# A two-layer graph transformer: order of the last products of a block, the engine of two bias adds, and the place of the last weight sums

## The chip, the cores and the metric

The kernel runs on one core of a Trainium2 chip. The core has five engines with a queue each, and each queue runs in order: TensorE (PE, matrix products into PSUM), VectorE (DVE), ScalarE (ACT), GpSimd (POOL) and SyncE (SP, which here only issues DMAs). The metric is the device time of one launch in microseconds; lower is better.

## The reference

`x` is 2708 x 512, `adj` a sparse symmetric 0/1 matrix of 2708 x 2708 (about 9 ones in a row, the diagonal included). Two layers follow each other, each a graph attention with 8 heads of 64 and a feed-forward part of 2048:

```
q, k, v = h @ Wq.T + bq, h @ Wk.T + bk, h @ Wv.T + bv
scores  = q . k / 8, -1e9 where adj (plus the diagonal) is 0
ctx     = softmax(scores) @ v
h1 = layer_norm(h + ctx @ Wo.T + bo, ln1_g, ln1_b)
ff = relu(h1 @ W1.T + b1) @ W2.T + b2
h2 = layer_norm(h1 + ff, ln2_g, ln2_b)
```

All is in 32-bit floats.

## The kernel before

The program is written engine by engine with a schedule by hand: what stands first in the code stands first in its engine's queue. The 22 tiles of 128 tokens are sorted by number of neighbours. For a tile, POOL gathers the rows of keys and values of each token's neighbours by indirect DMA (`kv`), VectorE multiplies and sums them (L1150, L1156), ScalarE forms the weights `p` and scales the values (L1169, L1176), and VectorE adds (L1182, L1189). This attention runs ahead of the feed-forward part and beside it: the generator `attend` is advanced by `advance` a little in each of the 16 steps f of a feed-forward block, by a table of paces.

A feed-forward block has two tiles, A and B (256 tokens side by side in `hT`). Step f makes 128 hidden units: four products `pf` on PE (L1653), then ScalarE's relu into `ft` (L1664). The main loop puts other work between the steps:

- in f = 5 to 8 the steps of `keys_values` for the block before: transposes of its result `z`, then for each tile the products k and v (`project`, L620). ScalarE copies both out of PSUM (L1735, L1739), POOL adds the bias `bk` to k afterwards (L1745) and then stores the rows by indirect DMA.
- in f = 5 `residuals` gathers the input rows `xb` of the next block; in f = 9 `settled_rows` has POOL add the bias `bo` to them (L1431).
- in f = 10 to 12 `attended` of the next block: transposes of the attention's result `cx`, the projection `o` of each tile on PE, `h = o + xb` on VectorE (L1456), the norm (L1265 to L1279, with a root on POOL, L1275).
- in f = 15 `turned`: eight transposes of these `h` into the next `hT`.

Small products `o`, k, v and transposes share PSUM buffers of the tag g, of which this stage has two.

In layer 0 the blocks 2 to 9 use `feed_forward_by_seven` for the second product with W2. Hidden units 2j and 2j+1 form pair j. For the pairs 0 to 6 the 2 x 2 block product (tokens A, B by the left and right half of the outputs, L and R) is done with seven products of 128 x 128 x 256 instead of eight (a Strassen-Winograd scheme). It needs sums of tokens, formed by VectorE per pair in `sums(j)` (L1625 to L1628, at f = 2j + 2), and sums of weights t2, t3, t4, formed once by `form(j)` in block 1, at the steps 3, 5, 7, 9, 13, 14 and 15, written to DRAM, and fetched anew for each pair of each block (`ask_forms`, L1610) into three fixed places, `self.slots`. These hold one pair, so the fetch for pair j + 1 goes out when the seven products of pair j have read them. The products go into four accumulators: a0, a1 (rows of A and B) and c0, c1 (shared parts). `products(j - 2)` stands at odd f. Pair 7 is plain: two products into a0 (128 x 512) and four into a1 (128 x 256).

A 128 x 128 x 256 product of floats is two PE instructions in the trace.

At a block's end the order on PE is: `pf` of f = 15, `products(5)`, the eight transposes of `turned`, `products(6)`, then the plain pair (L1674, L1678). ScalarE then copies c0's left half (u2, L1695), VectorE combines the accumulators with `h` (L1696 to L1703) and runs both norms. The next block's `pf` follow on PE at once; its `products(0)` stand at its f = 5.

Of the kernel before, what the change touches and what calls it, by code (L numbers as in the profile page):

```python
# [13 lines left out]
ALU = mybir.AluOpType  # L14
# [4 lines left out]
P = 128  # L19
DM = 512  # L20
# [5 lines left out]
NFC = FF // P  # L26
# [457 lines left out]
def by_edges(ctx: ExitStack, tc: tile.TileContext, x, xT, adj, layers, out, redo):  # L484
# [9 lines left out]
    nc = tc.nc  # L494
# [132 lines left out]
    def plus_rest(to, o, r, scale=None):  # L627
        for part in rest(o, r):
            if scale is None:
                nc.vector.tensor_tensor(to, part, to, ALU.add)  # L630
            else:
                nc.vector.scalar_tensor_tensor(to, part, scale, to, ALU.mult, ALU.add)
# [15 lines left out]
    def size(g):  # L648
        return min(P, N - g * P)
# [644 lines left out]
    class Layer:  # L1294
        def __init__(self, n, w):
            self.n, self.w, self.w1, self.w2, self.due = n, w, [], [], None
            self.apart, self.other = True, False
            self.with_bo = n > 0
            self.stores = nc.sync

        def load_first(self):
# [122 lines left out]
                xbs.append(xb)  # L1424
            return xbs

        def settled_rows(self, block, xbs):

            for g, xb in zip(block, xbs):
                r = size(g)  # L1430
                nc.gpsimd.tensor_tensor(xb[:r], xb[:r], self.bo[:r], ALU.add)  # L1431
            self.with_bo = True

        def attended(self, block, got, xbs=None):

            cTs, hs = [], []
            with_bo, self.with_bo = self.with_bo, self.n > 0

            def turn(g):
                r = size(g)  # L1440
                cx = got.pop(g)
                cT = dn.tile([P, NC, P], F32, tag="cT", name="cT", bufs=3)
                flip(cx, r, cT[:, :, :r], self.bv)
                cTs.append((g, r, cT))

            turn(block[0])
            xbs = xbs or self.residuals(block)
            yield
            if block == blocks[0]:
                turn(block[1])  # L1450
                yield
            for i, xb in enumerate(xbs):
                g, r, cT = cTs[i]
                o = project(lambda c: cT[:, c, :r], r, self.wo, "o")
                h = dn.tile([P, DM], F32, tag="h", name="h", bufs=4)
                nc.vector.tensor_tensor(h[:r], o[:r], xb[:r], ALU.add)  # L1456
                plus_rest(h[:r], o, r)
                if not with_bo:
                    nc.vector.tensor_tensor(h[:r], h[:r], self.bo[:r], ALU.add)
                norm(h, r, self.g1, self.e1b2)  # L1460
                hs.append(h)
                if len(cTs) == 1:
                    turn(block[1])
                yield
            yield hs
# [110 lines left out]
        def prepared(self):  # L1576

            place = wts.tile([P, NC, DM], F32, tag="wq", name="forms")
            place = place.rearrange("p c n -> p (c n)")
            W = 2 * P  # L1580
            self.slots = [place[:, i * W : (i + 1) * W] for i in range(3)]
            sums = place[:, 3 * W : 6 * W].rearrange("p (two s t) -> p two s t", two=2, t=P)
            self.sums = [sums[:, i] for i in range(2)]
            self.more_fts = [place[:, i * W : (i + 1) * W] for i in (6, 7)]
            self.asked = 0

        def form(self, j):

            w, W = self.w2[j], 2 * P
            b11, b12, b21, b22 = w[:, 0, :W], w[:, 0, W:], w[:, 1, :W], w[:, 1, W:]  # L1590
            t2, t3, t4 = self.slots
            nc.vector.tensor_tensor(t3, b22, b12, ALU.subtract)
            nc.vector.tensor_tensor(b12, b12, b11, ALU.subtract)
            nc.vector.tensor_tensor(t2, b22, b12, ALU.subtract)
            nc.vector.tensor_tensor(t4, b21, t2, ALU.subtract)
            for i, t in enumerate((t2, t3, t4)):
                nc.sync.dma_start(out=form_d[j, i], in_=t)
# [15 lines left out]
        def feed_forward_by_seven(self, k, block, hs, hT):  # L1613

            J, W = NFC // 2 - 1, 2 * P
            L, R = slice(0, W), slice(W, DM)
            a0, a1 = (ps_a.tile([P, DM], F32, tag=f"a{i}", name=f"a{i}") for i in range(2))
            c0, c1 = (ps_s.tile([P, DM], F32, tag=f"c{i}", name=f"c{i}") for i in range(2))
            fts = []
# [10 lines left out]
            def products(j):  # L1630
                f0, f1, w, s = fts[2 * j], fts[2 * j + 1], self.w2[j], self.sums[j % 2]
                t2, t3, t4 = self.slots
                first, last = j == 0, j == J - 1
                for to, left, right, start, stop in (
                    (a1[:, L], f1[:, P:], t4, first, False),
                    (c0[:, R], s[:, 1], t2, first, False),
                    (c1[:, L], f0[:, P:], t3, first, False),
                    (c0[:, L], f0[:, :P], w[:, 0, L], False, last),
                    (a0[:, L], f1[:, :P], w[:, 1, L], first, False),
                    (c1[:, R], s[:, 0], w[:, 0, R], False, last),  # L1640
                    (a0[:, R], s[:, 2], w[:, 1, R], False, False),
                ):
                    nc.tensor.matmul(to, left, right, start=start, stop=stop)  # L1643
                self.ask_forms(base + min(3 * j + 6, 3 * J + 3 * (k < NB - 2)))
                if k == NB - 2:
                    self.form_back(j)

            self.ask_forms(base + 3)
            for f in range(NFC):
                j = f // 2  # L1650
# [17 lines left out]
                if f % 2 and j > 1:  # L1668
                    products(j - 2)
                yield None  # L1670
            products(J - 1)
            for i in range(2):
                f, w = 2 * J + i, self.w2[J]
                nc.tensor.matmul(a0, fts[f][:, :P], w[:, i, :], start=False, stop=i == 1)  # L1674
            for cols in (L, R):
                for i in range(2):
                    f, w = 2 * J + i, self.w2[J]
                    nc.tensor.matmul(  # L1678
                        a1[:, cols],
                        fts[f][:, P:],  # L1680
                        w[:, i, cols],
                        start=False,
                        stop=(cols is R and i == 1),
                    )
            zA, zB = hs
            u2 = dn.tile([P, W], F32, tag="ft", name="u2", bufs=4)
            u34 = dn.tile([P, DM], F32, tag="row", name="u34", bufs=3)
# [20 lines left out]
        def keys_values(self, block, zs):  # L1708

            n = self.n + 1  # L1710
            kvs = at.tile([P, SLOTS, 2 * DM], F32, tag="kv", name="kvs", bufs=KVB)
            zTs = []

            def turn(i):
                g, z = block[i], zs[i]
                r = size(g)
                zT = dn.tile([P, NC, P], F32, tag="cT", name="zT", bufs=3)
                if r < P:
                    nc.gpsimd.memset(zT, 0.0)
                flip(z, r, zT[:, :, :r], self.nbo)  # L1720
                zTs.append(zT)

            turn(0)
            if block != blocks[-1]:
                turn(1)
            yield
            for i, (g, z) in enumerate(zip(block, zs)):
                r, zT = size(g), zTs[i]
                kv = kvs[:, i, :]
                k = project(lambda c: zT[:, c, :r], r, self.kv[0], "k")  # L1730
                if block == blocks[-1]:
                    nc.vector.tensor_tensor(kv[:r, :DM], k[:r], self.bk[:r], ALU.add)
                    plus_rest(kv[:r, :DM], k, r)
                else:
                    nc.scalar.copy(kv[:, :DM], k)  # L1735
                if len(zTs) == 1:
                    turn(1)
                v = project(lambda c: zT[:, c, :r], r, self.kv[1], "v")
                nc.scalar.copy(kv[:r, DM:], v[:r])  # L1739
                plus_rest(kv[:r, DM:], v, r)  # L1740
                nc.sync.dma_start(out=zT_d[n][g], in_=zT)
                nc.sync.dma_start(out=xb_d[n][g * P : g * P + r, :], in_=z[:r])
                yield
                if block != blocks[-1]:
                    nc.gpsimd.tensor_tensor(kv[:, :DM], kv[:, :DM], self.bk, ALU.add)  # L1745
            for i, g in enumerate(block):
                r = size(g)
                written[n].append(
                    put(kv_d[n], ident_i[:r, g : g + 1], kvs[:r, i, :], f"kv{n}")
                )  # L1750
            yield
# [130 lines left out]
    for n in range(NL):  # L1882
# [47 lines left out]
        for k, block in enumerate(blocks):  # L1930
# [14 lines left out]
            for f, zs in enumerate(working):  # L1945
# [16 lines left out]
                if more and f == NFC - 1:  # L1962
                    finish(asking)
                    hT = now.turned(blocks[k + 1], hs_next)
                if xbs and f == 9 + 2 * (k == 0):
                    now.settled_rows(blocks[k + 1], xbs)
                advance((PACE7 if seven else (PACE if k else PACES)[n])[f])
                if f in (0, 3, 7, 9) and (f or k):
                    next(asking, None)
# [116 lines left out]
```

## Time and profile before

| | us |
|---|---|
| median of 3 runs | 1870.61 (1869.64 to 1870.89) |
| the profiled execution, own time | 1877.7 |
| its span, first to last instruction | 1875.9 |
| stage of the eight seven-product blocks | about 397 to 1052 of the span |

In the profile PE, DVE, ACT and POOL are the engines, PEld is PE's loading of weights. A row of a group gives line, engine, operation, output<-inputs and shapes; "idle before" is how long the engine stood idle right before, and `<-` names what ended the wait. `forms` is the buffer that holds the slots, the token sums and two spare `ft` places, so `DMA forms<-form_d` is a fetch of weight sums, and `DVE forms L1627` a token sum. Line numbers are those of the kernel before; in the changed kernel lines from L1299 on are lower by 1 to 15.

### The profile page before, as it was taken

How to read it: one execution, taken by the hardware profiler on the slowest of the kernel's cores; microseconds unless marked ns; L12 is line 12 of the kernel's file. 1: busy time of each engine (PE TensorE's matmuls, PEld its weight loads, DVE VectorE, ACT ScalarE, POOL GpSimd, SP SyncE). 2: the span in 40 equal slices, each digit the busy share in tenths (PEclk: the TensorE clock that was granted, in tenths of full speed). 3: DMA queues.
4: the chain of work that ended last, by engine and by line, in shares of the span. 5: the costliest groups of instructions: out<-in, count | busy, mean ns of one | idle time of the engine just before them, and what ended most of it. 6: DMA issues, size and time to landing. Idle time of an engine off the chain costs nothing.

```text
span 1875.9 us, 22547 instructions
## 1 busy us (share of the span) xinstructions
PE 1827.0 (97%) x6563; PEld 1169.7 (62%) x6563; DVE 1461.5 (78%) x2407; ACT 960.7 (51%) x3291; POOL 860.4 (46%) x785
## 2 busy tenths in 40 slices
PE   9999999999989999998999999999999999999998
PEld 4444466566667767766776644566666666666666
DVE  5886778888788988878885336887989898998853
ACT  5760445545455565545644213456655675666541
POOL 3234755635454554645552114435544563555402
PEclk9999999999999999999999999999999999999999
DMA  9987976756665675656553568744736563654400
GB/s 345 370 327 270 369 262 229 252 172 212 207 206 181 204 248 195 208 196 193 182 175 110 177 226 326 276 156 160 254 129 226 197 238 131 226 209 165 145 23 21
DMA packets 158062, 393.82 MB, mean 210 GB/s; under 512 B 17514, under 2 KB 60894, under 8 KB 157928
## 3 DMA queue, kind: packets, MB, share of 16 engines
q0 software_dynamic: 70608, 252.12, 39.5%
q1 hardware_dynamic: 77162, 118.55, 18.5%
q10 hardware_dynamic: 10158, 21.61, 3.1%
q8 instruction: 54, 0.88, 0.2%
q14 instruction: 80, 0.66, 0.1%
HBM read 338.78 MB, written 53.44 MB: 209 GB/s over the span
## 4 chain that ended last, share of the span: by engine, by line
PE 48%; DVE 4%; ACT 2%; issue 1%; DMA 1%; POOL 0%; DVEq 0%; POOLq 0%
PE pf L1524 15%; PE a L1497 15%; PE o L620 5%; PE q L620 3%; PE pf L1653 2%; PE k L620 2%; PE v L620 2%; PE c L1643 1%; PE tp L1285 1%; PE a L1643 1%; ACT kv L1176 1%; DVE kv L1150 1%; DVE sc L1156 1%; DVE acc L1189 0%; PE a L1512 0%
## 5 line engine op out<-in xcount | busy, mean ns | idle before, releaser
L1113 POOL DMA_INDIRECT kv<-kv_d,listed x420 | 522.7, 1245 | 272.6 <-issue 93.2
L1524 PE MATMUL pf<-hT,w 128*128 128x256 f32 (+1 forms) x1792 | 393.2, 367 | 0.1
L1524 PEld LDWEIGHTS pf<-hT,w 128*128 128x128 f32 x1792 | 323.5, 190 | 103.2 <-issue 63.4
L1497 PE MATMUL a<-w,ft 128*128 128x512 f32 x800 | 373.1, 592 | 0.0
L1275 POOL TENSOR_TENSOR rd<-va,mhalf 128x1 f32<-128x1 f32 (+1 forms) x88 | 83.5, 948 | 522.3 <-DVE va L1273 522.1
L1176 ACT ACTIVATE kv<-kv,p 128x64 f32<-128x64 f32 x1232 | 311.0, 335 | 5.4
L1150 DVE TENSOR_TENSOR kv<-kv,q 128x1024 f32<-128x1024 f32 (+1 forms) x222 | 257.9, 1162 | 14.6 <-DMA q<-q_d,ident_i 12.9
L1156 DVE TENSOR_REDUCE sc<-kv 128x16 f32<-128x1024 f32 (+1 forms) x222 | 258.0, 1162 | 7.6
L1653 PE MATMUL pf<-hT,w 128*128 128x256 f32 x1024 | 236.8, 384 | 11.2 <-ACT ft L1664 11.2
L1189 DVE TENSOR_TENSOR acc<-acc,kv 128x1024 f32<-128x1024 f32 (+2 forms) x178 | 206.1, 1158 | 37.7 <-ACT kv L1176 21.3
L1653 PEld LDWEIGHTS pf<-hT,w 128*128 128x128 f32 x1024 | 194.6, 192 | 49.9 <-ACT ft L1664 13.4
L1497 PEld LDWEIGHTS a<-w,ft 128*128 128x128 f32 x800 | 150.1, 190 | 113.2 <-issue 101.3
L1535 ACT ACTIVATE ft<-pf,b 128x256 f32<-128x256 f32 (+1 forms) x208 | 95.0, 459 | 200.9 <-PE pf L1524 195.4
L1169 ACT ACTIVATE p<-sc,listed 128x8 f32<-128x8 f32 x420 | 104.4, 297 | 159.0 <-DVE sc L1156 147.1
L620 PE MATMUL o<-wo,cT 128*128 128x512 f32 x336 | 153.3, 600 | 8.4 <-DVE h L1456 6.7
L1182 DVE TENSOR_TENSOR kv<-kv,p 128x512 f32<-128x512 f32 (+1 forms) x178 | 130.5, 733 | 27.5 <-ACT p L1169 27.4
L1664 ACT ACTIVATE ft<-pf,b 128x256 f32<-128x256 f32 x96 | 44.7, 467 | 146.9 <-PE pf L1653 146.9
L620 PEld LDWEIGHTS o<-wo,cT 128*128 128x128 f32 x336 | 63.4, 192 | 85.4 <-issue 72.5
L745 DVE MAX8 tops<-code 128x8 f32<-128x247 f32 (+2 forms) x242 | 78.5, 400 | 28.0 <-ACT code L740 28.0
L1279 DVE SCALAR_TENSOR_TENSOR h<-h,rd,ln_b 128x512 f32<-128x512 f32 (+1 forms) x88 | 66.1, 751 | 42.5 <-POOL rd L1275 42.5
L1220 ACT ACTIVATE cx<-acc,su 128x64 f32<-128x64 f32 (+1 forms) x352 | 88.2, 333 | 15.3 <-DVE flags L1804 7.5
L1176 ACT ACTIVATE acc<-kv,p 128x64 f32<-128x64 f32 (+1 forms) x352 | 88.8, 334 | 1.4
(234 smaller groups left out, 2344.0 us busy)
## 6 DMA issues: line engine op xcount, KB each, us to landing
aj<-in_adj SPq DMA_DIRECT2D x42, 677.0 KB, 6.0
forms<-form_d SPq DMA_DIRECT2D x168, 128.0 KB, 3.6
kv_d<-kvs ACTq DMA_DIRECT2D x21, 512.0 KB, 5.4
xg<-in_xT SPq DMA_DIRECT2D x19, 512.0 KB, 7.6
w<-in_W SPq DMA_DIRECT2D x16, 512.0 KB, 6.8
kv<-kv_d,listed POOLq DMA_INDIRECT x420, 6.1
zT_d<-zT SPq DMA_DIRECT2D x22, 256.0 KB, 3.4
xb_d<-h SPq DMA_DIRECT2D x21, 256.0 KB, 4.6
```

Of the source, the lines that this page charges most:

```text
L620: nc.tensor.matmul(o[:r], xs(c), wm[:, c, :], start=(c == 0), stop=(c == NC - 1))
L1113: return nc.gpsimd.indirect_dma_start(out=to, out_offset=None, in_=table[:, :], in_offset=bass.IndirectOffsetOnAxis(ap=s, axis=0), bounds_ ...
L1150: nc.vector.tensor_tensor(kv[:r, :c, :DM], kv[:r, :c, :DM], self.q[:r].unsqueeze(1).to_broadcast([r, c, DM]), ALU.mult,)
L1156: nc.vector.tensor_reduce(self.sc[:r, s0 : s0 + c, :], kv[:r, :c, :DM].rearrange("p s (h d) -> p s h d", d=DK), AX.X, ALU.add,)
L1169: nc.scalar.activation(p[:r, s, :], self.sc[:r, s, :], AF.Exp, bias=minus[:r, g, s : s + 1])
L1176: nc.scalar.activation(to[:, i, hd], kv[:r, i, DM + h * DK : DM + (h + 1) * DK], AF.Copy, scale=p[:r, s0 + i, h : h + 1],)
L1182: nc.vector.tensor_tensor(to[:, 0, :].rearrange("p (h d) -> p h d", d=DK), kv[:r, 0, DM:].rearrange("p (h d) -> p h d", d=DK), p[:r, s0, : ...
L1189: nc.vector.tensor_tensor(self.acc[:r, :c, :], self.acc[:r, :c, :], kv[:r, :c, DM:], ALU.add)
L1497: nc.tensor.matmul(a[:r, cols], fts[f][:, c0 : c0 + r], self.w2[f // 2][:, f % 2, cols], start=(f == 0), stop=(f == NFC - 1),)
L1524: nc.tensor.matmul(pf[:, :w], self.w1[f // 2][:, c, f % 2 * P : f % 2 * P + P], hT[:, c, :w], start=(c == 0), stop=(c == NC - 1),)
L1535: nc.scalar.activation(ft[:, :w], pf[:, :w], AF.Relu, bias=self.b1[:, f : f + 1])
L1653: nc.tensor.matmul(pf[:, :W], self.w1[j][:, c, f % 2 * P : f % 2 * P + P], hT[:, c, :], start=(c == 0), stop=(c == NC - 1),)
```

## The change

Three things are changed.

1. In `feed_forward_by_seven` the plain pair's six products move ahead of `products(6)`; the flags that end an accumulation move with them.
2. The bias `bo` is no longer added to `xb` by POOL: `settled_rows` is gone, and in layer 0 VectorE adds `bo` to `h` for all blocks (before: the first block only). The bias `bk` is added by VectorE while it takes k out of PSUM, for all blocks (before: the last block only); ScalarE's copy of k and POOL's add go.
3. `form(6)` writes its sums to the three places where the token sums lie (`other_slots`), not to `self.slots`.

```diff
-            self.with_bo = n > 0
...
-        def settled_rows(self, block, xbs):
-            for g, xb in zip(block, xbs):
-                r = size(g)
-                nc.gpsimd.tensor_tensor(xb[:r], xb[:r], self.bo[:r], ALU.add)
-            self.with_bo = True
...
-                if not with_bo:
+                if self.n == 0:
                     nc.vector.tensor_tensor(h[:r], h[:r], self.bo[:r], ALU.add)
...
+            self.other_slots = [place[:, i * W : (i + 1) * W] for i in range(3, 6)]
...
-            t2, t3, t4 = self.slots
+            t2, t3, t4 = self.slots if j < NFC // 2 - 2 else self.other_slots
...
-                    (a1[:, L], f1[:, P:], t4, first, False),
+                    (a1[:, L], f1[:, P:], t4, first, last),
...
-                    (a0[:, R], s[:, 2], w[:, 1, R], False, False),
+                    (a0[:, R], s[:, 2], w[:, 1, R], False, last),
...
-            products(J - 1)
             for i in range(2):
                 f, w = 2 * J + i, self.w2[J]
-                nc.tensor.matmul(a0, fts[f][:, :P], w[:, i, :], start=False, stop=i == 1)
+                nc.tensor.matmul(a0, fts[f][:, :P], w[:, i, :], start=False, stop=False)
             for cols in (L, R):
...
-                        stop=(cols is R and i == 1),
+                        stop=False,
                     )
+            products(J - 1)
...
-                if block == blocks[-1]:
-                    nc.vector.tensor_tensor(kv[:r, :DM], k[:r], self.bk[:r], ALU.add)
-                    plus_rest(kv[:r, :DM], k, r)
-                else:
-                    nc.scalar.copy(kv[:, :DM], k)
+                nc.vector.tensor_tensor(kv[:r, :DM], k[:r], self.bk[:r], ALU.add)
+                plus_rest(kv[:r, :DM], k, r)
...
-                if block != blocks[-1]:
-                    nc.gpsimd.tensor_tensor(kv[:, :DM], kv[:, :DM], self.bk, ALU.add)
...
-                if xbs and f == 9 + 2 * (k == 0):
-                    now.settled_rows(blocks[k + 1], xbs)
```

More of the change, by code (lines that the diff above doesn't have):

```diff
@@ L1425, in residuals @@
             return xbs
-        def settled_rows(self, block, xbs):
-            for g, xb in zip(block, xbs):
-                r = size(g)
-                nc.gpsimd.tensor_tensor(xb[:r], xb[:r], self.bo[:r], ALU.add)
-            self.with_bo = True
         def attended(self, block, got, xbs=None):
             cTs, hs = [], []
-            with_bo, self.with_bo = self.with_bo, self.n > 0
             def turn(g):
```

## The prediction

> **What bounds the kernel now.** The page's first part comes first: which engine fills the span.
>
> ```profile
> PE 1827.0 (97%) x6563; PEld 1169.7 (62%) x6563; DVE 1461.5 (78%) x2407; ACT 960.7 (51%) x3291; POOL 860.4 (46%) x785
> ```
>
> TensorE (PE) sets the time. The change removes none of its products, so it can gain only where PE stands still or runs slowly. I cut the stage that it touches, the layer-0 blocks by seven products (397 to 1052 us), into its blocks (block ends read from the timeline of PE); columns: length, busy time of PE, PEld, DVE, ACT and POOL, granted clock, DMA share, GB/s.
>
> ```profile
> 316.40:397.00 80.60, 80.60 (x277) 50.03 (x276) 69.07 (x100) 44.62 (x164) 43.13 (x36) 1.00 0.68 220
> 481.60:567.10 85.50, 79.97 (x311) 58.06 (x310) 68.44 (x108) 41.79 (x153) 44.81 (x34) 0.96 0.60 193
> 567.10:644.20 77.10, 75.99 (x311) 56.61 (x311) 68.21 (x107) 43.80 (x162) 44.71 (x36) 1.00 0.69 226
> 807.00:892.40 85.40, 78.72 (x312) 57.64 (x311) 71.14 (x108) 46.00 (x171) 43.23 (x35) 0.98 0.59 186
> ```
>
> The plain block before (first row) has no idle PE. The seven-product blocks all have the same products, yet last from 77.1 to 85.5 us, and the long ones also had a lower clock. The waits of PE in 395 to 1052 us say on what (us in total, times, longest):
>
> ```profile
> PE pf L1653 <- ACT ft L1664: 11.2, 7, 3.6
> PE a L1643 <- DMA forms<-form_d: 9.9, 6, 2.7
> PE o L620 <- DVE h L1456: 6.7, 5, 2.4
> PE c L1643 <- DVE forms L1627: 4.1, 3, 2.9
> PE c L1643 <- DMA forms<-form_d: 2.3, 3, 1.1
> ```
>
> And the timeline of PE at one block's end shows where (start, us, what, idle before):
>
> ```profile
> 553.15 0.59 PE L1643 MATMUL a<-w,forms 128*128 128x256 f32 x2
> 553.58 1.04 PE L1285 MATMUL tp<-ident,h 128*128 128x128 f32 x8
> 556.46 0.89 PE L1643 MATMUL a<-forms,ft 128*128 128x256 f32 x2 [1.84 <-DMA forms<-form_d]
> 558.29 1.19 PE L1643 MATMUL c<-forms 128*128 128x256 f32 x2 [0.94 <-DMA forms<-form_d]
> ...
> 561.14 1.06 PE L1643 MATMUL a<-w,ft 128*128 128x256 f32 x2
> 561.99 1.06 PE L1643 MATMUL c<-w,forms 128*128 128x256 f32 x2
> 562.85 1.01 PE L1643 MATMUL a<-w,forms 128*128 128x256 f32 x2
> 563.69 1.88 PE L1674 MATMUL a<-w,ft 128*128 128x512 f32 x4
> 565.41 1.89 PE L1678 MATMUL a<-w,ft 128*128 128x256 f32 x8
> ```
>
> The last seven wait for weight sums that are fetched into slots which the seven before only just released: 0.87 us of transposes is all that lies between. After the wait PE starts a product every 0.85 us instead of 0.43, for some 4 us. The plain pair (3.44 us, needing no fetched sums) stands behind, where it covers nothing.
>
> **Part 1, the order of products.** One end without a wait is 0.87 of transposes, 7 x 0.43 and 3.44: 7.3 us, as the last two blocks show (965.20 to 972.54 and 1044.60 to 1051.91). The other six take 10.31, 13.55, 8.61, 9.47, 11.35 and 12.02 us: 21.3 over in all. Of this 12.4 is the waits themselves (11.4 on DMA, 1.0 on VectorE's token sums), the rest mostly half rate. In the new order the first sum is wanted 3.44 us later than the transposes' end, the next ones 0.43 and 0.86 after it. Against the landings seen: block of 556.46 wants at 557.89, its t2 that landed by 558.29 at 558.32; that of 884.04 at 884.65; that of 475.91 (third sum) at 476.48; the others have 1.3 us or more. So all are covered, three with 0.6 us or less to spare. Landings of these loads run from 1.8 to 6.3 us, so I charge 1.0 for one that comes late. The plain pair needs ft of f = 15: in the tightest block it ends at 797.02 and is wanted at 797.38. No charge. The moved step also issues, on SP's queue, the three fetches for the next block's first pair (in the last such block a reload of weights): 3.44 us later, for products that PE wants 10.4 us after the end; the landing of 3.5 (median) fits, and the stores behind them in the queue are waited for by nobody in this stage. No charge.
>
> Here the Trainium skill (TensorE: Matmul & The Clock Gate, "What's actually happening") weighs differently: the array falls to half clock after an idle window of about 3.4 us. No gap here is that long (the longest single one 2.66, two near each other 2.78 together), so by the rule each gap costs its own length: 12.4 us. By the row it costs 21.3. I take the row; the half-rate stretches at 558 and at 884 us follow gaps of 0.9 to 2.7 us.
>
> The price is the block's tail. The four accumulators used to be emptied partly beneath the plain pair; the last add chain began 0.2 us after the block's end E (481.82 against 481.62). Now c0's left half is ready at E - 1.1, ScalarE's copy takes 0.41 to reach VectorE, and the adds of the rows L1696 to L1700, each 0.33 to 0.61 apart, put L1701 at E + 1.87: 1.67 later. Behind it on VectorE stand the two norms, then the token sums of the next block's first pair, which PE wants at E + 10.8. Their third sum ended at E + 8.3 (489.92), so E + 10.0: 0.8 us of cover is left. Without it each boundary would wait.
>
> **Part 2, the biases.** POOL loses 20 adds of 1.38 us and 20 of 1.28; ScalarE 20 copies of 0.586. VectorE gains 20 of 0.69 (row of h<-h,bo) and 20 of 0.69 (kvs<-k,bk, which the last block has already): 27.6 us. But POOL's adds hold VectorE up. The timelines of POOL and of VectorE:
>
> ```profile
> 534.53 2.82 POOL L1431 TENSOR_TENSOR xb<-xb,bo 128x512 f32<-128x512 f32 x2
> ```
>
> ```profile
> 534.86 1.36 DVE L1625 TENSOR_TENSOR forms<-ft 128x128 f32<-128x128 f32 x1
> 536.26 1.25 DVE L1626 TENSOR_TENSOR ft<-ft 128x128 f32<-128x128 f32 x1
> 537.42 0.28 DVE L1627 TENSOR_TENSOR forms<-forms,ft 128x128 f32<-128x128 f32 x1
> ```
>
> Adds of 0.28 us took 1.36 and 1.25: 2.0 lost, just ahead of L1456, which frees the PSUM buffer that the second o projection waits for (at 538.85, 1.03). The same 2.0 to 2.1 stands ahead of the waits of 0.90, 0.19 and 2.21; another POOL add costs 1.55 (L1628, 1.84 for 0.29). Four waits go or nearly go: -4.3. The fifth (2.36, with 1.7 of half rate behind it) I leave: in that block VectorE never rests between the k adds and L1456, and 1.4 to 2.1 added meets 2.6 taken away.
>
> Each bo add lengthens the chain from o to the transposes of h by 0.69; those h are ready 2.7 us or more before PE wants them (632.93 against 635.62 is the closest), so nothing. A k add waits for PE's k. Queued behind it are scores and weights; but in seven of the eight blocks VectorE already waits 2 to 7 us there for ScalarE's p, which stands behind the copy of v, later than k. So its wait costs between 0 and, where nothing waits yet, 0.69; nothing, by the rows. It also frees k's PSUM buffer, which the next k wants 8.2 us after. In the block starting at 567.13 VectorE gets there at E + 26.6, with the tail E + 28.2, done at 28.9, while PE comes at 28.0: +1.0. The block from 892.4 already waits 0.18 for token sums: +1.0. ScalarE's lost copies are worth nothing, for the copy of v behind waits for PE anyway (31.1 us in 12 waits). Nor are POOL's: VectorE waits for no gather of keys in this stage.
>
> **Part 3, sums of the last pair.** The forming at 397.80 shows no wait, so other slots free nothing on VectorE. The first fetch can leave earlier; PE's 0.76 wait at 404.13 goes, but the wait of 2.87 behind it is for token sums and takes its place: 0, or -0.76 if it weren't so. Those sums are one bo add later: +0.7.
>
> **The sum**, on the profiled execution (1877.7 us, span 1875.9): -21.3 + 1.0 - 4.3 + 1.0 + 1.0 + 0.7 = -21.9. The median of the runs, 1870.61, is 7 us shorter; I take the same difference off it: 1849.
>
> **Rivals.** Forecast (0.80): most of the 21.3 is got; 1841 to 1861. The low end has all costs nought (-3.7) and the fifth o wait gone (-4.1); the high end has two thirds of the waits back in smaller size.
>
> Fetches stay late (0.09): if the ask meets busier queues and lands 2 us later, six ends still wait 1 to 1.5 us, partly with 1.7 of half rate: 12 to 15 given back, 1861 to 1865. For: the three margins. Against: SP's queue asks at the same point as before.
>
> The tail becomes the wait (0.11). PE would stop at the next block's first products, a place with 0.8 us of cover. If VectorE is 1.8 us later than I reckon, each of seven boundaries waits 1.0 and may add 1.7 of half rate: 19 given back, 1868, no change (0.06). From 2.8 us on, gaps of 2 us and half rate give back 26 and more: 1875 to 1880, slower (0.05). For: VectorE is 80 to 88% busy here. Against: its locks go, and POOL stands idle for the norms' reciprocal roots.
>
> POOL's locks not the cause: only the 4.3 is lost, 1853, within the forecast.
>
> 0.2% (3.7 us) is about what a measurement can tell. Faster 0.89, same 0.06, slower 0.05.
>
> **What would show it.** Ends of 7.3 us from the transposes to the next block's pf; no wait of L1643 on forms there; the blocks' clock 0.98 to 1.00; no DVE add of 0.28 us stretched above 1 us; fewer o waits on h. Wrong: waits of the first products on L1619 (token sums after), or k waiting for kvs.

## The result, and the profile after

| | us |
|---|---|
| before, median of 4 runs | 1870.12 (1867.2 to 1870.89) |
| changed, median of 4 runs | 1846.59 (1845.1 to 1851.91) |
| ratio | 0.9882, 95% interval 0.9859 to 0.9905 |
| profiled execution, own time (span) | 1845.1 (1843.4); before 1877.7 (1875.9) |

The change gains 23.5 us by the medians. The two profiled executions differ by 32.6; where the other 9 come from is shown below (the second look at the kernel before).

The page of the changed kernel, first part:

```profile
PE 1812.7 (98%) x6563; PEld 1164.1 (63%) x6563; DVE 1460.4 (79%) x2447; ACT 950.5 (52%) x3271; POOL 799.4 (43%) x745
```

PE has the same 6563 instructions and is busy 14.3 us less; nearly all of it is half rate that went (13.8 us in the ledger below). DVE has 40 instructions more, worth 27.6 us, and yet is busy 1.1 us less. So some 28.7 us of DVE's old busy time was not work but standing still inside its own instructions.

Three blocks of the changed kernel, with the columns of the prediction's table of blocks (they are the blocks of 85.5, 77.1 and 85.4 us before):

```profile
476.80:555.70 78.90, 76.50 (x312) 56.57 (x311) 67.55 (x113) 40.82 (x151) 37.30 (x30) 1.00 0.64 210
555.70:632.00 76.30, 75.74 (x312) 56.76 (x311) 68.89 (x113) 43.02 (x160) 39.28 (x32) 1.00 0.71 229
788.40:867.00 78.60, 76.34 (x312) 56.60 (x311) 68.70 (x108) 45.13 (x169) 36.91 (x31) 1.00 0.63 207
```

The long blocks are 6.6 and 6.8 us shorter, the one that was short already only 0.8, and the granted clock is 1.00 in all three. One of the ends on PE (the timeline, start first):

```profile
547.94 1.04 PE L1285 MATMUL tp<-ident,h 128*128 128x128 f32 x8
548.81 2.29 PE L1665 MATMUL a<-w,ft 128*128 128x512 f32 x4
550.94 1.89 PE L1669 MATMUL a<-w,ft 128*128 128x256 f32 x8
552.66 0.60 PE L1635 MATMUL a<-forms,ft 128*128 128x256 f32 x2
553.10 0.59 PE L1635 MATMUL c<-forms 128*128 128x256 f32 x2
...
555.25 0.59 PE L1635 MATMUL a<-w,forms 128*128 128x256 f32 x2
555.68 1.67 PE L1645 MATMUL pf<-hT,w 128*128 128x256 f32 x7
```

No row has a bracket, so nothing was waited for, and the sevens start every 0.43 us. From the transposes to the next `pf` it is 7.74 us (the 0.4 over 7.34 is one slower stretch of the plain pair, at full clock); the other ends take 7.34, or once more 7.74. What PE still waits for in 395 to 1052 us (total, times, longest):

```profile
PE pf L1645 <- ACT ft L1656: 9.5, 7, 2.2
PE c L1635 <- issue: 3.1, 1, 3.1
PE k L620 <- ACT zT L1290: 2.8, 5, 0.6
PE c L1635 <- DVE forms L1619: 1.0, 1, 1.0
PE a L1635 <- DVE h L1559: 0.8, 1, 0.8
```

Against before, all waits for fetched sums (12.2) and all five o waits (6.7) are gone. A wait of k for `zT` comes five times, 0.5 to 0.6 each; before there was one of 0.3. The 3.1 is the wait for the first token sums of the stage, the 0.8 just ahead of it the wait for an accumulator that VectorE's last add of block 1 (L1559) sets free. The 1.0 stands at the first products of the block from 866.95 us.

On VectorE the tail of a block (E = 476.76 here), in the timeline:

```profile
478.67 0.68 DVE L1693 TENSOR_TENSOR h<-a,h 128x512 f32<-128x512 f32 x1
...
486.46 0.28 DVE L1619 TENSOR_TENSOR forms<-forms,ft 128x128 f32<-128x128 f32 x1
```

L1693 is the old L1701. It starts at E + 1.91 and the third token sum ends at E + 9.98 (forecast 1.87 and 10.0). So it is in five of seven blocks; in two VectorE is still at its attention work at E, and the add starts at E + 2.7 and E + 3.9. And in VectorE's groups (count, busy in us, mean in ns, idle before in us), before in 462 to 985 us, then changed in 460 to 960 us:

```profile
L1182 DVE TENSOR_TENSOR kv<-kv,p 128x512 f32<-128x512 f32 x55 | 43.1, 784 | 18.1 <-ACT p L1169 18.1
L1626 DVE TENSOR_TENSOR ft<-ft 128x128 f32<-128x128 f32 x32 | 14.1, 439 | 1.1
```

```profile
L1182 DVE TENSOR_TENSOR kv<-kv,p 128x512 f32<-128x512 f32 x55 | 38.4, 698 | 4.1 <-ACT p L1169 4.1
L1618 DVE TENSOR_TENSOR ft<-ft 128x128 f32<-128x128 f32 x33 | 10.5, 319 | 1.1
L1723 DVE TENSOR_TENSOR kvs<-k,bk 128x512 f32<-128x512 f32 x12 | 8.2, 681 | 7.2 <-PE k L620 7.2
```

L1618 is the old L1626. The stretched adds are gone, and VectorE's wait for `p` has turned into a shorter one for k, as forecast.

So every mark that the prediction set for "right" is there. Of its marks for "wrong", the wait of the first products for token sums is there once (the 1.0). What the total doesn't show is whether each part is worth what its term said.

### The profile page after: what moved, and what is told of

Read it like the earlier page. It is cut to its first block, busy times and chain, and to the rows that moved or that the text cites. A ratio compares the mean times of both kernels' runs of the same rounds, so it can differ in the third digit from the quotient of the medians.

```text
span 1843.4 us, 22524 instructions
## 1 busy us (share of the span) xinstructions
PE 1812.7 (98%) x6563; PEld 1164.1 (63%) x6563; DVE 1460.4 (79%) x2447; ACT 950.5 (52%) x3271; POOL 799.4 (43%) x745
## 4 chain that ended last, share of the span: by engine, by line
PE 82%; DVE 9%; ACT 4%; issue 3%; POOL 2%; DMA 1%; POOLq 0%; SPq 0%; DVEq 0%
PE pf L1515 18%; PE a L1488 17%; PE k L620 8%; PE v L620 8%; PE q L620 8%; PE o L620 7%; PE pf L1645 5%; PE c L1635 4%; PE a L1635 2%; PE tp L1285 2%; ACT kv L1176 2%; DVE sc L1156 2%; DVE kv L1150 1%; POOL rd L1275 1%; DVE h L1279 1%
## 5 line engine op out<-in xcount | busy, mean ns | idle before, releaser
L1150 DVE TENSOR_TENSOR kv<-kv,q 128x1024 f32<-128x1024 f32 (+1 forms) x222 | 256.9, 1157 | 14.3 <-DMA q<-q_d,ident_i 11.0
L1182 DVE TENSOR_TENSOR kv<-kv,p 128x512 f32<-128x512 f32 (+1 forms) x178 | 123.3, 693 | 9.8 <-ACT p L1169 9.6
L1447 DVE TENSOR_TENSOR h<-o,xb 128x512 f32<-128x512 f32 (+1 forms) x44 | 30.3, 689 | 79.7 <-PE o L620 63.1
```

What stands on the lines that cost most here:

```text
L1150: nc.vector.tensor_tensor(kv[:r, :c, :DM], kv[:r, :c, :DM], self.q[:r].unsqueeze(1).to_broadcast([r, c, DM]), ALU.mult,)
L1182: nc.vector.tensor_tensor(to[:, 0, :].rearrange("p (h d) -> p h d", d=DK), kv[:r, 0, DM:].rearrange("p (h d) -> p h d", d=DK), p[:r, s0, : ...
```

## The experiments

The theory on trial is the prediction's sum: the order is worth 20 us, POOL's holds 4, `bk` and the places nothing. The main rival is that VectorE's later tail pays back part of the order's gain, and that the biases are worth more because they make room for it. The runs bear out the first half of it, at k, and not the second.

In each run below the ratio is to the kernel before on the same chip.

### The parts alone

The order alone: from the diff only the move of `products(J - 1)` behind the plain pair, with its flags.

```diff
-            products(J - 1)
             for i in range(2):
                 f, w = 2 * J + i, self.w2[J]
...
+            products(J - 1)
             zA, zB = hs
```

> Only the order of the last products, on the kernel before. Theory: the block ends carry the gain; the six slow ends shrink to 7.3 us each, the last seven wait for no fetched sum, and the kernel comes to about 1850 to 1855 (some 16 to 20 less). The waits of o for h and POOL's stretched VectorE adds stay. Rival (POOL's hold on VectorE is the larger part): 5 to 8 less at most, 1862 to 1866.

Measured: 1861.35 against 1871.97, ratio 0.9951 (0.9934 to 0.9968). That is 9 to 11 us, half of what its term said. PE's waits in 395 to 1052 us:

```profile
PE pf L1653 <- ACT ft L1664: 11.2, 7, 3.6
PE o L620 <- DVE h L1456: 8.5, 4, 4.6
PE c L1643 <- DVE forms L1627: 2.9, 1, 2.9
PE k L620 <- ACT zT L1290: 2.6, 3, 1.2
PE k L620 <- issue: 1.1, 2, 0.6
```

The waits for fetches are gone but for one of 0.8: the ends do what was forecast (1.2 us above 7.3 each, over all eight). But k, which before waited 0.3 once, now waits 3.7, and o 8.5.

The k waits are the tail's price. Set against the block's end, VectorE runs 1.6 to 2.3 us later at E + 14 than in the second trace of before (below), in six of seven blocks. ScalarE's `p` waits for VectorE's scores, the copies `zT` stand behind `p`, and so k comes 0.2 to 1.1 us later in six of seven blocks. VectorE makes the rest good by waiting less for `p`: at E + 39 it is later than before by no more than PE is, to within 0.5 us.

The o waits are another matter. All their growth is in one block, from 2.36 us in before to 4.65 here. In PE's timeline, and in the timelines of VectorE and POOL ahead of it:

```profile
933.29 5.37 PE L620 MATMUL o<-wo,cT 128*128 128x512 f32 x8 [4.65 <-DVE h L1456]
```

```profile
924.11 2.79 DVE L1182 TENSOR_TENSOR kv<-kv,p 128x512 f32<-128x512 f32 x1
```

```profile
923.85 2.49 POOL L1431 TENSOR_TENSOR xb<-xb,bo 128x512 f32<-128x512 f32 x2
```

Nothing of the tail is left here: at E + 19, and again at E + 42, VectorE is within 0.1 us of its times in the first trace of before. What differs is where POOL's adds fall. Here the two `bo` adds hold an add of 0.68 for 2.79, and a `bk` add has held one by 0.9 before that (at 917.41); in before the `bo` adds cost 1.07 in this block:

```profile
942.54 2.29 DVE L1150 TENSOR_TENSOR kv<-kv,q 128x1024 f32<-128x1024 f32 x1
```

Whether it is the order that moves the holds, or chance, one trace doesn't show. On top of it o takes 5.37 instead of 3.67.

The bias `bo` alone:

```diff
-                if not with_bo:
+                if self.n == 0:
                     nc.vector.tensor_tensor(h[:r], h[:r], self.bo[:r], ALU.add)
...
-                    now.settled_rows(blocks[k + 1], xbs)
```

> Only the bias bo on VectorE, on the kernel before. Theory: o waits for h at four to five places vanish, 3 to 6 less, 1864 to 1867; the ends wait for forms as before. Rival (POOL's hold is the larger part): 10 or more less. Rival (the add lengthens VectorE's chain): 0 to 5 more.

Measured: 1863.32, 0.9954 (0.9937 to 0.997): 8.6 us, twice the term. One o wait of the five is left in PE's waits:

```profile
PE o L620 <- DVE h L1447: 2.1, 1, 2.1
```

The bias `bk` alone:

```diff
-                if block == blocks[-1]:
-                    nc.vector.tensor_tensor(kv[:r, :DM], k[:r], self.bk[:r], ALU.add)
-                    plus_rest(kv[:r, :DM], k, r)
-                else:
-                    nc.scalar.copy(kv[:, :DM], k)
+                nc.vector.tensor_tensor(kv[:r, :DM], k[:r], self.bk[:r], ALU.add)
+                plus_rest(kv[:r, :DM], k, r)
...
-                if block != blocks[-1]:
-                    nc.gpsimd.tensor_tensor(kv[:, :DM], kv[:, :DM], self.bk, ALU.add)
```

> Only the bias bk on VectorE, on the kernel before. Theory: within 2 us of before, for its wait for k lies where VectorE waited for p anyway. Rival (a VectorE add that waits for PE holds up scores and token sums): 3 to 8 more. Rival (POOL's hold): 5 or more less.

Measured: 1868.31, 0.9982 (0.9967 to 0.9998): about 3 us, where the term said nothing. The o waits are 4.1 in its trace, against 6.7 and 7.4 in the two traces of the kernel before.

The places alone:

```diff
-            t2, t3, t4 = self.slots
+            t2, t3, t4 = self.slots if j < NFC // 2 - 2 else self.other_slots
```

> Only the other place for the last pair's weight sums, on the kernel before. Theory: within 1 us of before; the wait of 0.76 for a fetch at the start of the first block by seven goes, and the wait for token sums behind it takes its place. Rival: 1 to 4 less, if the fetch set that start.

Measured: 1871.96, 1.001 (0.9996 to 1.0024). Nothing, as forecast. With `bo` moved and the old places, PE waits 1.3 to 1.9 us for the stage's first fetch, with the new ones 0.6 to 0.8 for an accumulator at the same point; no run separates that.

Both biases, without the order:

> Both biases on VectorE, the old order and place. Theory (the o waits are what the biases are worth): no o wait on h over 0.5 us, the ends wait as before; as bo alone or 1 to 3 less, 1859 to 1864. Rival (each bias is worth its own gain): 12 less, 1860 or below, with k's part beside the o waits.

Measured: 1861.13 against 1870.86, 0.9945 (0.9931 to 0.9958). PE's waits in 395 to 1052 us:

```profile
PE a L1634 <- DMA forms<-form_d: 10.1, 8, 3.1
PE pf L1644 <- ACT ft L1655: 9.5, 7, 2.2
PE c L1634 <- DMA forms<-form_d: 4.3, 6, 1.6
PE c L1634 <- DVE forms L1618: 2.9, 1, 2.9
```

No o wait is left, the fifth included. PE's waits for fetches stay (14.4 us in the stage, 12.2 before), and `pf`'s wait for `ft` is 1.7 shorter, which no term had.

The order with `bo`, without `bk` and with the old places, and beside it the changed kernel again on the same chip:

> New order and bo on VectorE, bk left to ScalarE and POOL. Theory (the new order's later tail pushes VectorE back until o waits for h; bo's move makes this good): o waits vanish but for one, and 17 to 20 of the 23 us are there, 1850 to 1855. Rival (bk is needed for it): o waits stay above 4 us in all, 1855 to 1860.

> The changed kernel once more, beside the others on one chip: 1845 to 1850, and a second profile for the share of half rate (6 us in the first).

Measured: 1849.98 (0.9892, 0.9876 to 0.9908) and 1849.62 (0.9884, 0.9869 to 0.99). Beside the other two parts `bk` is worth too little for these runs to tell from nothing, though PE's waits fall from 20.6 to 17.4 us with it and the new places.

What follows: the order is worth 0.49%, the biases together 0.55%, the whole 1.16 to 1.18%. The parts add up within their intervals, and the two halves are about equal, not 20 to 4. That the biases make room for the order isn't shown: they are worth 0.55% without it and some 0.67% with it, which the intervals don't separate.

### The kernel before once more

> The kernel before once more, for a second profile. If the half-rate stretches behind PE's gaps follow the gaps alone, the same three ends show them; if they depend on when a gap falls, others do or none, and the span moves by some us with them.

Measured: 1868.26 (span 1866.4, clock 0.995 against 0.990). With this second trace the stage can be put in a ledger. Its length is taken from the first to the last start of a `pf`; the waits are the sum of PE's list in 395 to 1052 us; half rate is worked out from PE's timelines as the time by which products that start at twice their usual distance are late. The last column adds up the stretches of the stage in which the trace's granted clock is 0.50.

| kernel | stage | waits | half rate | at clock 0.50 |
|---|---|---|---|---|
| before, first trace | 648.4 | 35.1 | 20.2 | 30.7 |
| before, second trace | 640.6 | 35.4 | 12.2 | 13.7 |
| order alone | 634.0 | 27.8 | 13.5 | 20.5 |
| biases alone | 630.8 | 26.8 | 11.6 | 13.7 |
| changed | 616.6 | 17.2 | 6.4 | 6.8 |
| changed, second trace | 615.3 | 17.4 | 4.8 | 3.4 |

A stretch at clock 0.50 costs half its length at most; the other 3 to 5 us of "half rate" in each trace are products that start late at full clock. The two traces of before have the same waits and differ by 7.8 us in length, all of it half rate (8.0; by the clock 8.5). So the first trace, from which the prediction worked, was an execution with much half rate; that is most of the difference between 32.6 and 23.5. Its mean clock is 0.990, against 0.9934 over 23 runs of this kernel.

From the second trace to the changed kernel the stage is 24.0 shorter: 18.2 of waits and 5.8 of half rate, which closes. By place it is 18.2 at the ends, 8.0 at o and 1.8 at `pf`, less 2.8 at k and 1.6 at first products (23.6 in all).

For the order alone it is 6.6, where the ends give 17.9 (excess 19.1 to 1.2). Of the 11.3 lost again, k's waits are 3.7, longer o waits 1.2, half rate behind two o waits 3.5, and half rate at the stage's start, ahead of any end, 2.8. The last two are not the luck of this trace alone: over six runs of the order alone the mean clock is 0.9935, against 0.9934 in before. The half rate that left the ends came back elsewhere; why it did is not shown.

### Is it the gap, or the fetch?

The half rate behind a wait could come from the idle gap or from the DMA traffic. On the kernel before, four products whose results nothing uses fill the place where PE would wait:

```diff
+            pr = ps_f.tile([P, DM], F32, tag="f", name="pr")
+            for _ in range(4):
+                nc.tensor.matmul(pr[:, :W], ones, self.w1[J][:, 0, :], start=True, stop=True)
             products(J - 1)
```

> The kernel before with four products of ones (0.43 us each, results unused) between the transposes and the last seven, so that PE is busy while the fetches land. Theory (gaps of 1 to 2.8 us drop PE to half rate): no half-rate stretch at the ends; they exceed 7.3 us by the larger of wait and filler, 16.7 in all instead of 21.3: some 4 less than before. Rival (half rate has another cause, gaps cost only their length): the stretches stay and the ends come to 25: some 4 more.

Measured: 1872.14 against 1871.96, 1.001 (0.9999 to 1.002). PE's timeline at the end that the prediction showed:

```profile
552.07 1.89 PE L1673 MATMUL pr<-w,ones 128*128 128x256 f32 x8
554.51 0.70 PE L1643 MATMUL a<-forms,ft 128*128 128x256 f32 x2 [0.55 <-DMA forms<-form_d]
555.16 0.67 PE L1643 MATMUL c<-forms 128*128 128x256 f32 x2
555.67 0.59 PE L1643 MATMUL c<-forms,ft 128*128 128x256 f32 x2
```

And the granted clock behind the wait (columns as in the table of blocks), before and with the filler:

```profile
556.84:560.26 3.42, 2.48 (x6) 1.34 (x5) 1.84 (x6) 0.17 (x1) 0.00 (x0) 0.50 0.81 301
```

```profile
554.10:557.50 3.40, 2.99 (x13) 2.40 (x14) 2.54 (x7) 0.89 (x3) 0.01 (x1) 1.00 0.73 270
```

The sum is still late by 0.55, but the products go on at 0.43 to 0.65, and the clock is 1.00 under much the same DMA traffic; at no end of this trace is it lower. So the half rate goes with PE's idle time, not with the fetch. The ends are shorter, as expected (17.0 above 7.3 each, over all eight, the filler counted, against 19.1 to 21.4 before), and the time is no better all the same. Where it went the trace shows only in part: the o waits, counted alike (with one of 0.6 to 0.7 that the lists put down to `ft` or to no releaser), are 9.8 us against 7.3 and 8.0 in the two traces of before, and the clock is at 0.50 for 13.7 us, no less than in the second of these, but at the stage's start and behind o and `pf` instead of at the ends.

### Two ways on

Of the waits left, the largest is `pf` for `ft` (9.5). The step of `keys_values` at f = 7 puts ScalarE's copy of v into its queue ahead of the attention's steps, and the copy waits there for PE. In the changed kernel the step goes behind `advance`:

```diff
-                if f in (5, 6, 7, 8) and behind:
+                if f in (5, 6, 8) and behind:
                     next(behind)
...
                 advance((PACE7 if seven else (PACE if k else PACES)[n])[f])
+                if f == 7 and behind:
+                    next(behind)
```

> The changed kernel, with the second tile's k and v and their evictions put behind the attention step of f = 7 instead of ahead of it. If the waits of PE's pf for ScalarE's ft (9.5 us in 7) come from ScalarE's and VectorE's standing still until v is there, they fall to 3 or less and the kernel to 1835 to 1842. If they come from the amount of ScalarE's work, no change.

Measured: 1835.33 against 1871.96, 0.9807 (0.9792 to 0.9822), 11 to 14 below the changed kernel's two medians. ScalarE's waits in 395 to 1052 us, the changed kernel first, then this one:

```profile
ACT kvs L1728 <- PE v L620: 94.0, 17, 9.4
```

```profile
ACT kvs L1728 <- PE v L620: 48.0, 13, 8.5
```

Half of ScalarE's standing still for v is gone, and `pf`'s wait for `ft` falls from 9.5 to 0.8.

On top of it, the last seven in another order, those that need no fetched sum first:

```diff
-                for to, left, right, start, stop in (
+                seven = [
...
-                ):
+                ]
+                if last:
+                    seven = [seven[i][:4] + (i in (6, 0, 1, 2),) for i in (3, 4, 5, 6, 0, 1, 2)]
+                for to, left, right, start, stop in seven:
```

> As the swapped one, and of the last seven products of a block the four that need no fetched sum go first, so that c0's left half is ready 1.3 us sooner and the fetches have 1.7 us more. If the later tail costs anything (waits of k for zT 3.0, token sums 1.0), 1 to 4 less than the swapped one; if not, the same.

Measured: 1840.49, 0.9839 (0.9823 to 0.9856): 5 slower than without it. The fetches at the ends were covered already, and the tail starts later, not sooner. ScalarE's copy of c0's left half, in the version before it (E = 475.14) and in this one (E = 476.70):

```profile
474.04 0.37 ACT L1687 COPY u<-c 128x256 f32<-128x256 f32 x1 [1.00 <-PE c L1635]
```

```profile
476.47 0.37 ACT L1690 COPY u<-c 128x256 f32<-128x256 f32 x1 [1.87 <-PE c L1638]
```

The left half is ready at 474.27, but the copy starts when the product into c0's right half ends (476.43), and that one now stands last but one. So the tail begins 0.9 us later against E. The first weights `p` of the next block on ScalarE, in the same two:

```profile
487.87 0.49 ACT L1169 ACTIVATE p<-sc,listed 128x8 f32<-128x8 f32 x2 [0.45 <-DVE sc L1156]
```

```profile
490.29 0.49 ACT L1169 ACTIVATE p<-sc,listed 128x8 f32<-128x8 f32 x2 [1.31 <-DVE sc L1156]
```

E + 12.7 against E + 13.6. The copies `zT` stand behind `p` in ScalarE's queue, and k behind them waits 1.20 instead of 0.55 there. Over the stage k's waits are 6.0 instead of 2.8, and 1.1 us of new waits for fetches come in mid-block. This shows the way by which a later tail gets to PE: VectorE's scores, ScalarE's `p`, `zT`, k.

Last, the stage's first token sums (3.1 and 0.8). At the end of block 1 both adds that set the accumulators free go first, and only the first tile's norm stays ahead of the sums; the second goes behind, in `sums`. This too is on top of the moved step.

```diff
+            self.late = []
...
+            if self.n == 0 and block == blocks[FORMED]:
+                for a, h in zip(accs, hs):
+                    nc.vector.tensor_tensor(h, a, h, ALU.add)
+                norm(hs[0], P, self.g2, self.e2)
+                self.late = [hs[1]]
+                yield list(hs)
+                return
...
                     sums(j - 1)
+                    while self.late:
+                        norm(self.late.pop(), P, self.g2, self.e2)
```

> The swapped kernel (second tile's k and v behind the attention step of f = 7), with the second norm of the last plain block put behind the first token sums of the block after it. Theory: the wait of 3.1 for these sums and of 0.6 to 0.8 for the freeing of a1 goes, with the half rate behind it: 4 to 7 less than the swapped kernel, 1828 to 1832. Rival (the norm is then late for the transposes of z): the same or more.

Measured: 1830.35 against 1870.86, 0.9784 (0.9771 to 0.9797), the best of all, 4 to 5 below the moved step alone. PE's waits in 395 to 1052 us come to 5.1 in all, the largest being:

```profile
PE k L620 <- ACT zT L1290: 2.8, 5, 0.6
PE c L1643 <- DVE forms L1627: 0.9, 1, 0.9
PE pf L1653 <- ACT ft L1664: 0.8, 1, 0.8
```

## Why the prediction was right, and where its terms were not

The time was right (1849 forecast, 1846.59 measured). The sum came out because two errors of opposite sign cancel, the order worth half its term and the biases worth twice theirs. That is luck.

- **The ends, -21.3 and +1.0 for a late fetch.** The mechanism holds: the ends came down to 7.3 us, and no fetch was late. But the term took the first trace's half rate as typical; with the second trace it is 19. And a gain at the ends isn't yet a gain in time: alone, the order is worth 9 to 11 us.
- **The tail, no charge.** Its delay was sized right (E + 1.91, E + 9.98 in most blocks), the place where it would be paid was not. The prediction looked at the next block's first products and at their 0.8 us of cover. They held, but for 1.0 once, in the block whose tail starts at E + 3.9; the prediction did charge 1.0 for this block, but for a wait in mid-block. The tail was paid for at k, some 17 us behind the block's end: 3.7 us with the order alone, 2.8 in the changed kernel. This is the step that failed though the number came out. The rival "the tail becomes the wait" named this price, at the wrong place and far too high.
- **The biases, -4.3, and nothing for `bk`.** Mis-sized: they measured about 10 together (`bo` 8.6, `bk` 3). All five o waits went, the fifth too, and 1.7 of `pf`'s waits. The prediction left the fifth because VectorE "never rests" there, so that 1.4 to 2.1 us of added work would meet 2.6 of holds taken away. But its own trace has VectorE rest 1.91 for q at 922.05, behind the first k add, which takes that add up. With both biases VectorE reaches this L1456 2.8 us sooner than before, set against the block's end, where PE had waited 2.36. The relief comes from this block: at E + 32 VectorE is within 0.4 us of where it was before. By the page, holds of 28.7 us went for adds of 27.6, so the gain is in the time at which the work is done, not in its amount.
- **k waiting for its PSUM buffer, +1.0.** It didn't happen. k waits for `zT` instead, five times some 0.56, which no term had (2.8 in all, the tail's price).
- **The first sums, +0.7.** 0.82 and 3.06 against 0.76 and 2.87 before: +0.25. The fetch wait went, as forecast, and one for an accumulator took its place. The last norm of block 1 set them, as the last run shows.
- **The places, nothing.** Right, alone.

Open is what `bk` is worth beside the other two parts, and whether the parts do more together than their sum: from 0.49% and 0.55% to 1.16 to 1.18% is within the intervals.

## What to carry to other kernels

A stall taken from the engine that sets the time is worth in full only where the engine next to it can keep up: before the sum is closed, ask by how much the change makes that second engine later or earlier, and follow it through the whole block to each place where the first one meets it, not only to the next. A delay of that engine is often made good at its own waits, so it has to be followed in the trace and not carried on by assumption. And a term that contains half rate should be taken from more than one execution: two traces of the same kernel had the same waits and differed by 8 us.

## What the runs showed of the hardware

A gap's length alone doesn't tell whether TensorE falls to half rate behind it. In the second trace of before, o ran at full rate (3.67) behind a gap of 2.19, in PE's timeline; with the order alone it took 5.37 behind one of 1.91:

```profile
860.02 3.67 PE L620 MATMUL o<-wo,cT 128*128 128x512 f32 x8 [2.19 <-DVE h L1456]
```

```profile
851.26 5.37 PE L620 MATMUL o<-wo,cT 128*128 128x512 f32 x8 [1.91 <-DVE h L1456]
```

Behind the same gap of 3.06 at 408 us half rate began at once in the kernel with the moved step and in the second trace of the changed kernel, and 1 us later in its first. A gap of 3.6 of `pf` at 1003 to 1018 us brought it in all five traces that have one, a gap of 1.90 at the same place in none of five.

What decides is where the gap lies on a grid of time. In the fourteen traces the stretches at clock 0.50 in this stage are 3.41 or 6.83 us long, and within a trace they begin and end on one grid of 3.41 us. Two cells of that grid around these gaps (columns as in the table of blocks), the second trace of before and then the order alone:

```profile
858.61:862.02 3.41, 2.00 (x5) 1.06 (x6) 2.67 (x6) 0.00 (x0) 2.78 (x3) 1.00 0.61 195
862.02:865.43 3.41, 3.41 (x13) 2.27 (x12) 3.17 (x8) 0.00 (x0) 0.07 (x1) 1.00 0.47 166
```

```profile
848.68:852.10 3.42, 1.51 (x6) 0.73 (x5) 3.21 (x7) 0.59 (x2) 2.96 (x3) 1.00 0.57 202
852.10:855.51 3.41, 3.41 (x5) 1.33 (x4) 2.54 (x7) 0.00 (x0) 1.19 (x2) 0.50 0.80 275
```

A gap that two cells share leaves PE busy enough in both (here 2.00 of 3.41, and 2.64 in the cell ahead); one that falls within a cell doesn't (1.51), and the next cell runs at 0.50. Counted from 392 to 1046 us in the fourteen traces, 43 of 2630 cells at full clock are followed by one at 0.50. PE was busy for at most 0.50 of each of the 43, and every cell in which it was busy for less than 0.41 is among them; in between both happen. The grid lies differently in each execution, so the same gap costs its own length in one and 1.7 us more in another. The Trainium skill (TensorE: Matmul & The Clock Gate, "What's actually happening") ties the fall to an idle window of about 3.4 us and says that the windows run freely. The grid bears out the free-running window of 3.4 us; the window needn't be idle here, so the measurement decides.

A GpSimd add of two inputs held a VectorE add of two inputs: 2.79 us instead of 0.68 in the order-alone run, while POOL's two adds ran (923.85 to 926.34), counted as VectorE's busy time. Such a hold shows only as a mean that is too long for its shape, never as a wait.
